# Four node-graph pairs beside the last sort and four in two alternating series after it

## The chip, the cores and the metric

The kernel runs on one core of a Trainium2 chip. The metric is the device time of one execution in microseconds (us); lower is better. The engines named here are PE (TensorE: matmuls, and PEld for the loads of their weights), DVE (VectorE), ACT (ScalarE), POOL (GpSimd, which also issues indirect DMAs) and SP (SyncE, which issues most plain DMAs).

## What is computed

There are 16 graphs of 1024 nodes with 64 channels, an adjacency matrix for each, and a node mask. Two layers follow each other, each with a residual. Cut to what matters:

```python
# layer 0
h = relu(layernorm(x))
# drop some neighbours of nodes with many, then for every node and channel
# sort the values of its neighbours and take three quantiles:
agg = sum(w * quantile(sorted_neighbours(h), tau) for tau, w in ((.25,.25), (.5,.5), (.75,.25)))
x = x + (relu((h + agg) @ W1 + b1) @ W2 + b2) * nodemask
# layer 1
h0 = relu(layernorm(x))
for i in (1, 2, 3):                      # three graph convolutions
    h_i = bn_i(relu(adj @ (h_{i-1} @ W_i) + b_i))
x = x + relu(concat(h_1, h_2, h_3) @ Wl + bl)
```

The expensive part is the sort of the neighbours' values. Layer 1 multiplies by the whole adjacency matrix of a graph three times.

## The kernel before

**Pairs and stages.** Two graphs of 64 channels fill the 128 partitions, so the 16 graphs are eight pairs, 0 to 7. For every pair, `prepare` turns the adjacency into lists of live neighbours, and puts the nodes in an order of their number of neighbours (`place` is that order). Nodes of similar number make a block; there are seven blocks (0 to 6) and the last 16 nodes, the tails, which are sorted for several pairs at once (`sort_tails`: here for pairs 4 to 7 together). `gather_block` brings a block's neighbour values with one-hot matmuls on PE (pg, L1018) whose right-hand sides s are compared on DVE (L987); ACT copies the result (g, L1023). `sort_block` sorts with minima and maxima on DVE (L935 to L950) and sums the quantiles into agg. `store` transposes the sums on PE (pt_agg, L1043), copies them on ACT (o, L1051) and writes them to the DRAM tensor agg_d (L1053).

**The later layers.** The rest of layer 0 and the whole of layer 1 are `later`, which is a generator: it yields between pieces, and whoever steps it decides where in the program's order its next piece lies. For a pair p it consists of two parts.

- `first(p)`, five steps. It loads xt (L1240) and h (L1241) with DMAs of SP, brings agg back in the nodes' own order with 16 indirect gathers of POOL, 128 rows each (L1243), and loads the mask bytes mk (L1249). Then `first_layer` adds agg and h on DVE (L1142), transposes on PE (pt, L1131), multiplies by W1 and W2 (pm L1151, py L1155), adds bias, mask and residual (h L1156, L1158, L1159), runs layer 1's layernorm on DVE and ACT (L560 to L568), and transposes again.
- `second(p)`, eleven steps. It loads the pair's two adjacency matrices (adjT, L1259, from SP), and `next_layer` does the three convolutions. For each it multiplies by W_i (pw, L1184) and splits the result into three bf16 parts (xw, L1185 to L1190). Two halves of 48 matmuls by the adjacency follow (pg, L1200), each with its relu on ACT (xT, L1204) and scaling on DVE (xT, L1205). The last linear layer is pf (L1216), then bias (L1220), relu and residual (res, L1223), and the store to out (L1225).

Within `later`, the steps of second(p) and first(p+1) alternate. All its tiles come from a pool "late" with one buffer each (only xt has two), and a PSUM pool with two buffers of each of its two tags.

**The order of the work.** Each engine works in program order. `weave` walks the sort's steps and, by the share of the sort that is done, steps other generators between them. While the sorts of pairs 0 to 6 run, these others are the preparation of the next pair and the gathers of the next block. The sort of pair 7, the last, has nothing left to prepare, so `later` runs there: in each of the seven blocks and the final one, `weave` spends STEPS = 7 steps of `later`, 56 in all. That is 5 for first(0), 3×16 for second(0) to second(2) with the first parts of pairs 1 to 3, and three steps of second(3). Between block 0 and block 1 the tails of pairs 4 to 7 are sorted, with block 1's gathers beside them. After the last sort `send` stores the last sums, and `ahead.rest()` does what remains of `later`, in the same order and the same pools. A check on inputs out of the usual (a flag, from L1504) ends the program.

Of the kernel before, what the change touches and what calls it, by code (L numbers as in the profile page):

```python
# [19 lines left out]
PSUM = bass.MemoryType.PSUM  # L20
# [8 lines left out]
TAUS = ((0.25, 0.25), (0.5, 0.5), (0.75, 0.25))  # L29

SHARES = (10, 9, 17, 24, 20, 13, 0)
STEPS = 7

MAGIC = 8388608.0

# [366 lines left out]
def graph_layers_kernel(ctx: ExitStack, tc: tile.TileContext, ins, out: bass.AP):  # L402
# [6 lines left out]
    NP = NB // 2  # L409
# [144 lines left out]
    def rows_of(ap):  # L554
        return ap.rearrange("(t p) c -> p t c", p=P)
# [550 lines left out]
    def weave(sort, *others):  # L1106


        share, taken = 0.0, [0] * len(others)

        def due(share):
            for i, (steps, count, first, end) in enumerate(others):
                while taken[i] < count and first + (end - first) * taken[i] / count <= share:
                    steps.step()
                    taken[i] += 1

        due(0.0)
        for part in sort:
            share += part
            due(share)  # L1120
        due(1.0)
# [15 lines left out]
    def first_layer(pools, xt, h, agg, mask):  # L1137


        one, ps = pools  # L1140
        X = xt.shape[2]
        nc.vector.tensor_tensor(agg, agg, h, ALU.add)  # L1142
        oT = channels_first(pools, agg, "chan")
        yield
        for x in range(X):
            rows = slice(x * C, (x + 1) * C)
            hT = one.tile([HID, N], F32, tag="hT", name="hT")
            for hf in range(NH):
                sl = slice(hf * HALF, (hf + 1) * HALF)
                pm = ps.tile([HID, HALF], F32, tag="mm", name="pm1")  # L1150
                nc.tensor.matmul(out=pm, lhsT=w1[rows, :], rhs=oT[rows, sl], start=True, stop=True)  # L1151
                nc.scalar.activation(hT[:, sl], pm, AF.Relu, bias=b1)
            py = ps.tile([P, NT, C], F32, tag="mm", name="py")
            for t in range(NT):
                nc.tensor.matmul(out=py[:, t, :], lhsT=hT[:, t * P : (t + 1) * P], rhs=w2, start=True, stop=True)  # L1155
            nc.vector.tensor_tensor(h[:, :, x, :], py, b2[:, None, :].to_broadcast([P, NT, C]), ALU.add)  # L1156
            yield
        nc.vector.tensor_tensor(h, h, mask[:, :, :, None].to_broadcast([P, NT, X, C]), ALU.mult)  # L1158
        nc.vector.tensor_tensor(xt, xt, h, ALU.add)  # L1159
        flat = "p t x c -> p (t x) c"  # L1160
        layernorm_relu(one, agg.rearrange(flat), xt.rearrange(flat), h.rearrange(flat), NT * X)
        yield
        return channels_first(pools, agg, "chan")
# [61 lines left out]
            nc.sync.dma_start(out=rows_of(graphs[x]), in_=res[:, :, x, :])  # L1225
        yield

    def later(pools, done):

        one, ps = pools  # L1230

        def first(p):
            assert p < done.sent
            xt = one.tile([P, NT, 2, C], F32, tag="xt", bufs=2, name="xt")
            h, agg = (one.tile([P, NT, 2, C], F32, tag=k, name=k) for k in ("h", "agg"))
            mk = one.tile([P, NT, 2], U8, tag="mk", name="mk")
            mask = one.tile([P, NT, 2], F32, tag="mask", name="mask")
            for x in range(2):
                b = 2 * p + x
                nc.sync.dma_start(out=xt[:, :, x, :], in_=rows_of(x_d[b]))  # L1240
                nc.sync.dma_start(out=h[:, :, x, :], in_=rows_of(h_d[b][:, :]))  # L1241
                for t in range(NT):
                    nc.gpsimd.indirect_dma_start(  # L1243
                        out=agg[:, t, x, :],
                        out_offset=None,
                        in_=agg_d[b][:, :],
                        in_offset=bass.IndirectOffsetOnAxis(ap=place[:, b, t : t + 1], axis=0),
                    )
                nc.sync.dma_start(out=mk[:, :, x], in_=mask_d[b])  # L1249
            yield  # L1250
            nc.vector.tensor_copy(mask, mk)
            cur = yield from first_layer(pools, xt, h, agg, mask)
            return xt, cur

        def second(p, x2, cur):
            adjT = []
            for x in range(2):
                adjT.append(one.tile([P, NT, N], F8, tag=f"adjT{x}", name=f"adjT{x}"))
                nc.sync.dma_start(out=adjT[x], in_=adjT_d[2 * p + x][:, :, :])  # L1259
            yield  # L1260
            yield from next_layer(pools, [out[2 * p], out[2 * p + 1]], adjT, x2, cur)

        given = yield from first(0)
        for p in range(NP):
            now = Steps(second(p, *given))
            ahead = Steps(first(p + 1)) if p + 1 < NP else None
            while now.step():
                yield
                if ahead is not None and ahead.step():
                    yield  # L1270
            if ahead is not None:
                ahead.rest()
                given = ahead.result
# [146 lines left out]
    with ExitStack() as stack:  # L1420
        keep = stack.enter_context(tc.tile_pool(name="keep", bufs=1))
        pools = (
            stack.enter_context(tc.tile_pool(name="work", bufs=1)),
            stack.enter_context(tc.tile_pool(name="ps", bufs=1, space=PSUM)),
            stack.enter_context(tc.tile_pool(name="rows", bufs=1)),
        )
        last = len(BLOCKS)
        with ExitStack() as inner:
            early = (
                inner.enter_context(tc.tile_pool(name="early", bufs=1)), keep,  # L1430
                inner.enter_context(tc.tile_pool(name="ps_early", bufs=1, space=PSUM)),
            )
            ahead = Steps(prepare(0, early))
            ahead.rest()
            st = ahead.result
            first, *_ = gather_block(st, 0, pools)
            first.rest()
            for p in range(NP - 1):


                def coming(st, p):
                    yield from st.number
                    return (yield from prepare(p + 1, early))

                ahead = Steps(coming(st, p))
                for n in range(last):
                    steps = (ahead, SHARES[n], 0.0, 1.0)
                    if n == 0 and p in TAILS:

                        tails = sort_tails(*TAILS[p], pools)  # L1450
                        next(tails)
                        weave(sort_block(st, n, pools), steps)
                        weave(tails, gather_block(st, n + 1, pools))
                    elif n == last - 1:
                        ahead.rest()
                        to_come = ahead.result
                        weave(sort_block(st, n, pools), gather_block(to_come, 0, pools))
                    elif n == last - 2:
                        weave(
                            sort_block(st, n, pools), gather_block(st, n + 1, pools),  # L1460
                            gather_block(st, last, pools, (early[0], "a", 2)), steps,
                        )
                    else:
                        weave(sort_block(st, n, pools), gather_block(st, n + 1, pools), steps)
                st = to_come
            for _ in st.number:
                pass


        with ExitStack() as inner:  # L1470
            one = inner.enter_context(tc.tile_pool(name="late", bufs=1))
            late = (one, inner.enter_context(tc.tile_pool(name="ps_late", bufs=2, space=PSUM)))
            done = Pair()
            done.sent = TAILS[NP - 1][0]
            ahead = Steps(later(late, done))
            for n in range(last + 1):
                steps = (ahead, STEPS, 0.0, 1.0)
                if n == 0:
                    tails = sort_tails(*TAILS[NP - 1], pools)
                    next(tails)  # L1480
                    weave(sort_block(st, n, pools), steps)
                    weave(tails, gather_block(st, n + 1, pools))
                    continue
                if n < last:
                    weave(sort_block(st, n, pools), gather_block(st, n + 1, pools), steps)
                else:
                    weave(sort_block(st, n, pools), steps)
                done.sent = NP - 1
            send(pools)
            done.sent = NP  # L1490
            ahead.rest()


    with ExitStack() as stack:
# [43 lines left out]
```

## Time and profile before

| What | Value |
|---|---|
| Runs | 3160.47, 3166.65, 3176.45 us, median 3166.65 |
| The profiled execution | 3163.56 us, its span 3161.8 us |
| Mean granted clock of TensorE | 0.915 of full |
| PE busy over the span | 2599.2 us (82%) |
| DVE busy over the span | 2559.8 us (81%) |
| ACT / POOL busy | 1696.2 / 619.5 us |
| Last sort (pair 7), from its first work to its last sum | 2376.6 to 2832.1 us of the span |
| Residual stores' last operation (L1223) of pairs 0 to 7 | 2622.5, 2734.9, 2821.7, 2898.8, 2971.5, 3046.9, 3107.6, 3153.7 us |
| The convolutions' matmuls (L1200) | 2304 matmuls, 284.5 us busy |
| The gathers of agg (L1243) | 128, 171.2 us busy |

Busy shares are means over the whole span; the change touches only the last quarter of it, so the table's positions matter more than its shares. Times of single operations are their start on the span's clock. A wait in the profile is put down to the one thing that came last.

### The profile page before, as it was taken

The numbers are of one execution on the slowest core, as the hardware profiler recorded it, in microseconds if no ns is written. First come the engines' busy times: TensorE is split into PE (matmuls) and PEld (weight loads), VectorE is DVE, ScalarE is ACT, GpSimd is POOL, SyncE is SP. The second block draws the span as 40 slices with busy tenths as digits, with TensorE's granted clock in tenths as the row PEclk, the third lists the DMA queues.
The fourth block names the chain that finished last, engine by engine and source line by source line (L and its number), as shares of the span: only waits on it lengthen the run. The fifth ranks groups of instructions, "written<-read, shape, count | busy, mean of one in ns | idle before, by whom it ended". The sixth has DMA issues, their size and how long they took to land.

```text
span 3161.8 us, 67201 instructions
## 1 busy us (share of the span) xinstructions
PE 2599.2 (82%) x27849; PEld 1697.4 (54%) x27849; DVE 2559.8 (81%) x5895; ACT 1696.2 (54%) x3292; POOL 619.5 (20%) x545
## 2 busy tenths in 40 slices
PE   2678978898888889885798889888986688977778
PEld 1445655565556556653565566456643456644445
DVE  4149889998999799989998999899976979963332
ACT  4764666567557755774367557745853223332221
POOL 5110161022102200330022103300422530311110
PEclk9779999999899999997899999999987799988989
DMA  4131022111211212122111211211113011122211
GB/s 138 46 104 60 3 67 70 56 55 52 66 57 54 64 56 68 46 72 47 42 64 51 66 56 57 67 56 63 48 36 75 9 41 26 49 55 54 54 54 42
DMA packets 221082, 177.45 MB, mean 56 GB/s; under 512 B 189024, under 2 KB 189152, under 8 KB 216672
## 3 DMA queue, kind: packets, MB, share of 16 engines
q1 hardware_dynamic: 141824, 125.88, 13.1%
q0 software_dynamic: 17408, 37.81, 3.9%
q10 hardware_dynamic: 61536, 9.39, 1.7%
q8 instruction: 219, 3.59, 0.5%
q14 instruction: 95, 0.78, 0.1%
HBM read 124.44 MB, written 48.55 MB: 55 GB/s over the span
## 4 chain that ended last, share of the span: by engine, by line
DVE 40%; PE 29%; ACT 12%; DMA 8%; issue 6%; another core or an unknown queue 2%; POOL 2%; ACTq 1%; DVEq 0%; POOLq 0%; SPq 0%
PE pg L1018 11%; DVE t L935 10%; DVE s L987 9%; DVE g L935 8%; PE pg L1200 5%; ACT junk L770 3%; DMA a<-in_adj 3%; DMA lp<-live_d 3%; DVE junk_v L673 2%; PE pr L845 2%; DVE g_tails L935 1%; DVE t_tails L935 1%; PE keys L763 1%; PE pf L1216 1%
## 5 line engine op out<-in xcount | busy, mean ns | idle before, releaser
L1018 PE MATMUL pg<-s,hp 128*64 128x400 bf16 (+11 forms) x16848 | 1366.5, 313 | 172.3 <-DVE s L987 138.1
L1018 PEld LDWEIGHTS <-hp 128*64 128x64 bf16 x16848 | 894.5, 112 | 553.9 <-issue 109.6
L987 DVE TENSOR_SCALAR s<-r 128x3200 bf16<-128x3200 bf16 (+25 forms) x1312 | 623.6, 521 | 103.6 <-PE pg L1018 74.9
L778 POOL DMA_INDIRECT live_d<-edge,place x128 | 261.1, 2040 | 1354.3 <-DVE place L773 1149.9
L1023 ACT COPY g<-pg 128x400 f32<-128x400 f32 (+10 forms) x384 | 169.0, 443 | 399.4 <-PE pg L1018 363.1
L935 DVE TENSOR_TENSOR t<-g 128x600 f32<-128x600 f32 (+9 forms) x524 | 315.5, 626 | 34.0 <-ACT g L1023 33.2
L1200 PE MATMUL pg<-adjT,xw 128*64 128x512 fp8e4 x2304 | 284.5, 398 | 52.8 <-ACT xw L1185 25.7
L935 DVE TENSOR_TENSOR g<-t 128x96 f32<-128x96 f32 (+16 forms) x555 | 283.2, 537 | 1.2
L1243 POOL DMA_INDIRECT agg<-agg_d,place x128 | 171.2, 1338 | 495.2 <-PE pt L1131 258.2
L671 ACT ACTIVATE edge<-a 128x1024 fp8e4<-128x1024 f32 x128 | 135.1, 1058 | 214.4 <-DMA a<-in_adj 213.9
L1200 PEld LDWEIGHTS <-xw 128*64 128x64 bf16 x2304 | 140.1, 114 | 182.4 <-issue 42.0
L868 ACT ACTIVATE coef<-z,bias 128x200 f32<-128x200 bf16 (+6 forms) x480 | 173.9, 405 | 102.3 <-DVE agg L950 66.0
L935 DVE TENSOR_TENSOR t<-t 128x192 f32<-128x192 f32 (+20 forms) x447 | 207.8, 475 | 0.2
L871 ACT ACTIVATE coef<-coef,wcol 128x200 f32<-128x200 f32 (+7 forms) x512 | 189.6, 403 | 9.3 <-issue 7.1
L673 DVE SCALAR_TENSOR_TENSOR junk_v<-a 128x1024 fp8e4<-128x1024 f32 x128 | 155.4, 1214 | 24.4 <-DMA a<-in_adj 24.4
L845 PE MATMUL pr<-liveT,upto 128*128 128x512 fp8e4 (+2 forms) x384 | 127.4, 350 | 53.1 <-ACT r L851 46.9
L770 ACT ACTIVATE junk<-keys,minus 128x1024 fp8e4<-128x1024 f32 x128 | 144.3, 1128 | 38.1 <-PE keys L763 34.3
L851 ACT CAST r<-pr 128x592 bf16<-128x592 f32 (+1 forms) x256 | 142.5, 585 | 41.1 <-PE pr L847 32.1
L794 POOL DMA_DIRECT2D lp<-live_d x128 | 89.4, 699 | 376.9 <-PE pt L809 319.3
L812 ACT ACTIVATE liveT<-pt 128x1024 fp8e4<-128x1024 f32 x128 | 130.3, 1034 | 50.5 <-PE pt L809 47.1
L752 ACT ACTIVATE edge<-q,bias 128x1024 fp8e4<-128x1024 f32 x128 | 141.8, 1108 | 22.6 <-PE q L747 22.6
L725 ACT ACTIVATE stays<-cs,back 128x1024 f16<-128x1024 f32 x128 | 136.7, 1111 | 31.1 <-PE cs L721 15.9
(182 smaller groups left out, 3879.4 us busy)
## 6 DMA issues: line engine op xcount, KB each, us to landing
a<-in_adj SPq DMA_DIRECT2D x128, 512.0 KB
adjT_d<-edgeT SPq DMA_DIRECT2D x16, 1024.0 KB
lp<-live_d POOLq DMA_DIRECT2D x128, 128.0 KB
adjT<-adjT_d SPq DMA_DIRECT2D x16, 1024.0 KB
room<-in_x SPq DMA_DIRECT2D x16, 256.0 KB
h_d<-room SPq DMA_DIRECT2D x16, 256.0 KB
h_again<-h_d SPq DMA_DIRECT2D x16, 256.0 KB
xt<-in_x SPq DMA_DIRECT2D x16, 256.0 KB
```

Of the source, the lines that this page charges most:

```text
L673: nc.vector.scalar_tensor_tensor(junk, a, 1.0, a, ALU.is_equal, ALU.not_equal, accum_out=odd[:, b, t : t + 1], saturate=False)
L770: nc.scalar.activation(junk, keys, AF.Sign, bias=minus[:, t : t + 1], accum_out=above[:, t : t + 1], saturate=False)
L778: sent = nc.gpsimd.indirect_dma_start(out=live_d[b][:, :], out_offset=bass.IndirectOffsetOnAxis(ap=place[:, b, t : t + 1], axis=0), in_=ed ...
L845: nc.tensor.matmul(out=pr[:, o], lhsT=upto, rhs=liveT[:, u, sl], start=True, stop=(u == 0))
L868: nc.scalar.activation(coef[:, i, :], z[:, at], AF.Abs, bias=bias(rank - (slots + 1) // 2 + tau), scale=sign)
L871: nc.scalar.activation(coef[:, i, :], coef[:, i, :], AF.Relu, bias=wcol[:, q : q + 1], scale=-w)
L935: nc.vector.tensor_tensor(view(bufs, o, n1, n2), view(bufs, a, n1, n2), view(bufs, b, n1, n2), ALU.max if op else ALU.min)
L987: nc.vector.tensor_scalar(s[:, k, :, us, w0:], r[:, :, us, at + w0 : at + W], float(LIVE + 1 + k0 + k), None, ALU.is_equal)
L1018: summed = nc.tensor.matmul(out=pg[x * C : (x + 1) * C, ks, w0:], lhsT=st.hp[:, part, x, u, :], rhs=s[:, ks, x, u, w0:], start=(whole and ...
L1023: nc.scalar.copy(g[:, k0 : k0 + n, :], pg)
L1200: nc.tensor.matmul(out=pg[cs, :], lhsT=part[:, u, cs], rhs=adjT[x][:, u, sl], start=(u == 0 and k == 0), stop=(u == NT - 1 and k == len(xw ...
L1243: nc.gpsimd.indirect_dma_start(out=agg[:, t, x, :], out_offset=None, in_=agg_d[b][:, :], in_offset=bass.IndirectOffsetOnAxis(ap=place[:, b ...
```

## The change

Two constants, `later`'s arguments and the end of the program change:

- `later` gets a list of pairs. Beside the last sort it runs pairs 0 to 3 (BESIDE = 4), in the order that it had.
- STEPS is 9, but block 0 gets one step only. That is 1 + 7×9 = 64 steps, which are the 5 + 3×16 + 11 of four whole pairs.
- After the last sort's stores, all pools of the sort and of these pairs are closed. New pools are opened, "last" with two buffers of each tile and "ps_last" with four buffers of each of its two tags, and `later` runs there with `apart` on.
- With `apart` two generators are made, one for pairs 4 and 6 and one for pairs 5 and 7. Each does first(p) and second(p) of its pairs one after the other, and they are stepped in turn, one step each.

```diff
-STEPS = 7
+STEPS = 9
+
+BESIDE = 4
...
-    def later(pools, done):
+    def later(pools, done, pairs, apart=False):
...
-        given = yield from first(0)
-        for p in range(NP):
+        def in_turn(pairs):
+            for p in pairs:
+                yield from second(p, *(yield from first(p)))
+
+        if apart:
+            both = [Steps(in_turn(pairs[k::2])) for k in range(2)]
+            while any([one.step() for one in both]):
+                yield
+            return
+        given = yield from first(pairs[0])
+        for p in pairs:
             now = Steps(second(p, *given))
-            ahead = Steps(first(p + 1)) if p + 1 < NP else None
+            ahead = Steps(first(p + 1)) if p + 1 in pairs else None
...
-            ahead = Steps(later(late, done))
+            ahead = Steps(later(late, done, range(BESIDE)))
             for n in range(last + 1):
-                steps = (ahead, STEPS, 0.0, 1.0)
+
+                steps = (ahead, STEPS if n else 1, 0.0, 1.0)
...
             send(pools)
-            done.sent = NP
             ahead.rest()
+
+
+    with ExitStack() as stack:
+        done.sent = NP
+        late = (
+            stack.enter_context(tc.tile_pool(name="last", bufs=2)),
+            stack.enter_context(tc.tile_pool(name="ps_last", bufs=4, space=PSUM)),
+        )
+        Steps(later(late, done, range(BESIDE, NP), True)).rest()
```

## The prediction

> **What bounds the kernel now.** I first read busy times by stage (columns: stretch, its length, busy time and count of PE, PEld, DVE, ACT, POOL, then granted PE clock, DMA share, GB/s). The last sort runs from 2376.6 to 2832.1, its last store's transpose pt_agg starts at 2832.4, and the span ends at 3161.8. That split carries the sum below.
>
> ```profile
> 2376.60:2440.60 64.00, 41.50 (x271) 24.16 (x267) 37.92 (x50) 17.08 (x42) 18.36 (x16) 0.65 0.45 84
> 2440.60:2491.00 50.40, 18.27 (x179) 13.76 (x177) 50.40 (x207) 12.60 (x44) 37.04 (x15) 0.68 0.10 22
> 2491.00:2527.80 36.80, 36.30 (x369) 23.05 (x367) 36.52 (x53) 12.29 (x28) 3.59 (x2) 0.97 0.04 3
> 2527.80:2606.00 78.20, 69.66 (x772) 47.25 (x767) 56.90 (x80) 21.63 (x47) 26.66 (x16) 0.98 0.12 28
> ...
> 2863.00:2885.00 22.00, 9.69 (x47) 4.63 (x49) 4.38 (x6) 3.10 (x5) 10.34 (x11) 0.63 0.08 18
> 2885.00:3155.00 270.00, 230.40 (x1817) 145.96 (x1813) 87.71 (x123) 64.51 (x104) 30.21 (x32) 0.93 0.19 54
> ```
>
> Rows 1 and 2 are block 0 and the tails of the sort, rows 3 and 4 blocks 1 and 2; in rows 1 and 2 PE is much idle, in row 3 PE and DVE are both full. After the sort (last two rows) PE is busy 85% and DVE 32%: PE is the bound there, except in row 5, the gather of one pair. In steps of 5 us:
>
> ```profile
> 2865.00:2870.00 5.00, 1.42 (x8) 1.12 (x8) 0.57 (x1) 0.69 (x1) 3.78 (x5) 0.87 0.12 26
> 2870.00:2875.00 5.00, 2.34 (x9) 0.72 (x9) 1.38 (x2) 1.20 (x2) 3.78 (x5) 0.50 0.12 26
> 2875.00:2880.00 5.00, 0.09 (x2) 0.09 (x4) 0.11 (x1) 0.59 (x1) 1.08 (x2) 0.50 0.06 13
> 2880.00:2885.00 5.00, 5.00 (x24) 2.04 (x26) 2.31 (x3) 0.62 (x1) 0.00 (x0) 0.50 0.00 0
> ```
>
> Here PE starves (about 11 us lost) and its clock halves. Why the gather is late stands in the waits of 2832 to 3156, and what it does beside the sort in those of 2376 to 2832 (engine, line and what it waited for: us, times, longest):
>
> ```profile
> POOL agg L1243 <- PE pt L1131: 167.9, 3, 57.9
> ```
> ```profile
> DVE agg L1142 <- DMA agg<-agg_d,place: 22.6, 2, 12.6
> ```
>
> POOL waits until a pair's transposes pt free the only agg tile; then its 16 gathers start, too late for the next pair's first layer. The tail thus costs 77.1, 72.7, 75.4, 60.7 and 46.1 us from one res (L1223) to the next (2821.7, 2898.8, 2971.5, 3046.9, 3107.6, 3153.7): 46.1 is a pair alone, 60.7 adds a first layer (14.6), 75 adds a late gather (about 15).
>
> **What the skill says.** (1) "TensorE: Matmul & The Clock Gate", Part 1: an array idle for a window of about 3.4 us drops to half clock and needs as much busy time to return. The trace agrees: 0.50 after 2870. (2) "DMA: Bandwidth & Descriptors", SWDGE vs HWDGE vs iDMA: software on GpSimd writes the descriptors of GpSimd's DMAs, in SBUF, where DVE can lock it out. In the trace one gather is 0.94 us busy with 0.30 us between (16 take 20 us) in the tail, but a group beside the sort takes 29 to 45 us, single ones up to 10.3. (3) "Trainium Architecture — The Big Picture", Inside one NeuronCore: each engine has its own stream, meeting others at semaphores. A wait thus holds everything behind it; L1142 waiting 12.6 us for a gather is that. (4) "Trainium Kernel Development and Optimization", Best Practices: double-buffer to overlap DMA with compute. The single agg agrees with the need; whether it helps depends on what runs meanwhile.
>
> **The change, part by part.** The instruction order of the changed program shows that it does what it says: pairs 0 to 3 end with the sort (64 steps = 5 + 3×16 + 11; before 56, which stopped inside pair 3), then two series alternate on PE in groups of 48 matmuls. Five places move time.
>
> A. *Block 0 gets one step.* The one step issues pair 0's loads and gathers; mask and L1142 still stand in block 0 on DVE, but pair 0's first-layer PE work and layernorm leave it. Before, L1142 ran at 2415.1 (gathers 2390.5 to 2413.4), and the block ended at 2440.3. Behind L1142, the sort needs only 5.4 us of coefficient work: end about 2421.7, **−18.6**.
>
> B. *Tails.* Three layernorm operations (1.22 each) go: 3.65 of an all-DVE stage (50.40 of 50.40): **−4.0** with their waits.
>
> C. *Block 1.* Pair 0's layernorm (six operations of about 1.2, 7.1 us) comes here, and pair 1's gathers, which wait for pair 0's transposes, can start only near 2500 where before they ran under the tails. With the 27.5 us of a disturbed group they land near 2530, while DVE reaches L1142 of pair 1 near 2513; behind it stand the s operations (L987) that PE needs, so both stop: 17 us. Two further steps bring PE about 9 us. 17+7+9 = **+33**. Bounds: 16 if the gathers take 20 us and half the PE work fits; 50 for a 45 us group.
>
> D. *Blocks 2 to 7*, 304.4 us before. Half a pair more: 195 pg matmuls at 10.6 us per 96 are 21.6, pw 4: 25.6 us of PE work at 85% (PE was 87% busy here): +22. Pair 2's late gather (12.6) goes, pair 3's now meets DVE: about +16, by the nearest waits (12.6, and C). Sum **+25**; bounds +4 (work fits in the 40 us of idle PE, gathers cancel) and +42. So pt_agg comes at 2832.4−18.6−4+33+25 ≈ **2868**.
>
> E. *After the sort.* 329.4 us before. The new pools take the room of all older ones, so the first loads and the 32 gathers of pairs 4 and 5 wait for the last stores (o, agg_d): about 3.5 us after pt_agg. Call this G.
> - 32 gathers × 1.25 = 40, landing 46. Only pair 3's last work covers (pg 10.6, pf 5.6). PE's order puts pair 5's transposes among pair 4's first layer, so both wait for both gathers. Then two first layers with nothing beside: pair 0's took 37 us from L1142 to first xw at a low clock; two overlap in about 37. pg of pair 4 starts at G+**83**.
> - Seconds of 4 and 5: two of 3×10.6 + 2×2.0 + 5.6 = 41.4 are 83, the waits at layer ends hidden by the other series. But L1142 of pair 7 stands on DVE ahead of pair 4's second half of a layer (L1205); 32 gathers again take 40, DVE is released about 17 after PE wants it. 83+17+3 = **103**.
> - First layers of 6 and 7: both series are in the same phase, nothing lies beside: **38**.
> - Seconds of 6 and 7: 83+3 = **86**; res 2; out DMA to the end 7 (3154.9 to 3161.8 before), flag chain L1504 about 1: **10**.
> 3.5+83+103+38+86+10 = 323.5: **−6**. Bounds: −55 (second item's 17 and third item's 38 hidden) and +30 (groups of 32 at beside-the-sort pace).
>
> DMA queues: SP issues the same xt, h, mk, adjT and out transfers; adjT L1259 has a second buffer and comes earlier, priced nothing because pg never shows it as a releaser. Sizes don't change. PSUM gets four buffers for two: nothing, since both series use two each. ACT goes from 24% busy in the tail and is no bound.
>
> Sum: −18.6−4+33+25−6 = **+29** on the span of 3161.8, so 3191. The profiled execution took 3163.6, and its like after the change 3193; the median of the three shown, 3166.65, lies 3 higher (3160 to 3176), so I predict **3195**. About 0.5%, 16 us, is what a measurement of this kernel can tell from no change.
>
> **Rivals.**
> *1. No difference.* D fits into PE's idle time (+4 for +25) and C's gathers take 20 (−7): 3195−28 = **3167**. For it: PE is idle 42 us in blocks 1 to 7. Against it: DVE is full in several of those blocks (45.50 of 45.50 in 2659.8 to 2705.3), so idle PE time is largely waiting that added DVE work lengthens.
>
> *2. Faster: the second series really covers the first.* Place: the end of the seconds of 4 and 5. If the transposes of 6 and 7 run under those seconds, as "ahead" did before, and DVE isn't held by L1142, 17+38 = 55 go: **3140**. It decides when more than 45 of those 55 are hidden. For it: before, next pairs' first layers cost 14.6 each in place of 37. Against it: the two series are at the same step always, so both are in first layers together.
>
> *3. Much slower: gathers.* 32 in a row at the pace of pair 1's group beside the sort (45 us for 16) would cost some 40 more in the tail or in C and D: **3230**. For: single gathers of up to 10.3 us. Against: the tail's DVE is mostly idle, and there 16 took 20 us three times.
>
> *4. It does not do what it says.* One series is held by the other's tiles, as with one buffer; about 3195 + 2×15 = 3225, folded into 3.
>
> **How the numbers follow.** Main case 0.46 (3180 to 3212), rivals 3 and 4 0.23, rival 1 0.18, rival 2 0.13. The range 3156 to 3234 takes in the bounds of C and D, all of rival 1 and most of rival 3, leaving out rival 2 and a little. Same sign: slower by over 0.5% is main and rival 3, 0.69; same 0.18; faster 0.13.
>
> **What would show it.** Pair 0's L1142 near 2415 and block 0's end near 2422 (A); L1142 of pair 1 waiting about 17 on its gather (C); pt_agg at 2855 to 2885 (D); the first gather of the last pools 3 to 5 after it, then a stretch of 60 to 80 us with PE under 40% busy at half clock, and a second one of some 40 us (E). It is wrong if pt_agg stays near 2835, or if gathers of 6 and 7 are never a releaser of DVE, or if PE is over 85% busy from pt_agg+90 to the end.

## The result, and the profile after

The changed kernel took 3177.38 us (median of 12 runs, 3164.47 to 3190.50) against 3166.95 for the kernel before (12 runs, 3149.85 to 3180.10). The ratio is 1.0028, 95% interval 1.0004 to 1.0051: some 9 us slower, where 29 were forecast, and 3195. The direction was right, but barely: the interval begins at 1.0004, and a later group of runs gave 1.0013 (0.9993 to 1.0032). The size forecast was three times too large. Some 9 us is less than the 16 that the prediction held for the least that can be told from no change.

The profiled execution took 3174.97 us, its span is 3173.2. First its busy times by stage (stretch, length, busy time and count of PE, PEld, DVE, ACT, POOL, granted PE clock, DMA share, GB/s), from the last sum ahead of block 0 on: block 0, the tails, blocks 1 and 2.

```profile
2371.00:2416.50 45.50, 24.34 (x187) 13.33 (x189) 31.63 (x42) 14.36 (x37) 19.20 (x16) 0.66 0.59 115
2416.50:2461.30 44.80, 26.62 (x217) 17.22 (x215) 44.80 (x199) 11.41 (x41) 0.00 (x0) 0.72 0.01 2
2461.30:2523.40 62.10, 40.45 (x422) 26.42 (x420) 45.42 (x64) 16.24 (x38) 19.12 (x16) 0.79 0.10 19
2523.40:2575.50 52.10, 51.70 (x549) 37.79 (x546) 51.15 (x69) 16.72 (x35) 0.55 (x1) 1.00 0.07 12
```

Block 0 is short and block 1 long, as steps A and C said: PE is idle 21.65 of block 1's 62.10 us, 16.3 of them behind DVE, which waits for pair 1's gathers. Then the same view after the sort:

```profile
2855.00:2880.00 25.00, 5.78 (x15) 4.11 (x15) 1.23 (x1) 0.00 (x0) 19.21 (x20) 0.50 0.26 68
...
2942.00:2964.00 22.00, 6.12 (x12) 1.27 (x10) 1.23 (x1) 0.00 (x0) 16.09 (x17) 0.50 0.12 26
2964.00:3033.00 69.00, 67.17 (x578) 37.28 (x578) 17.66 (x28) 16.66 (x28) 0.00 (x0) 0.94 0.07 25
...
3062.00:3073.00 11.00, 0.59 (x3) 0.59 (x4) 10.93 (x13) 2.42 (x3) 0.00 (x0) 0.59 0.00 0
```

Rows 1 and 2 lie beside 32 gathers each; a stretch in which PE gets little done is called a bubble here. Row 4 is the layernorm of pairs 6 and 7 with nothing beside it: DVE full, PE empty. Row 3 shows what two series do when nothing disturbs them: PE is 97% busy. The surprise is in row 2. PE is not stopped there: it starts 12 matmuls in 22 us, none of which needs a gather. The waits after the sort (engine, line and what it waited for: us, times, longest) say the same:

```profile
ACT xT L1206 <- remote: 77.5, 2, 40.2
PEld L1202 <- issue: 38.9, 35, 2.7
PEld pf L1218 <- issue: 29.1, 23, 2.5
DVE agg L1144 <- DMA agg<-agg_d,place: 27.0, 2, 14.0
```

"issue" is time in which PE waited for nothing that the profile shows, and "remote" a signal whose sender it does not show. Beside the gathers PE's instructions, matmuls and weight loads, start in multiples of 0.70 us after one another (2950.91, 2952.31, 2953.01, 2954.41, ...), and the half layers' completions reach ACT late (first line). I call this the **crawl**.

Both kernels had a second profile taken in a later group of runs (before_again, after_again). With all four, the prediction's steps measure as follows. Block ends are starts of the last sum (L950, after the change L952); "last store" is pt_agg.

| Step | Forecast | First pair of profiles | Second pair |
|---|---|---|---|
| A, block 0 | -18.6 | 60.3 to 45.5: -14.8 | 60.2 to 44.8: -15.4 |
| B, tails | -4 | 50.6 to 44.8: -5.8 | 50.5 to 44.9: -5.6 |
| C, block 1 | +33 | 36.6 to 62.1: +25.5 | 43.2 to 62.5: +19.3 |
| D, blocks 2 to 7, to the last store | +25 | 305.0 to 311.7: +6.7 | 304.2 to 298.2: -6.0 |
| E, from there to the end | -6 | 329.3 to 338.1: +8.8 | 323.3 to 325.8: +2.5 |
| Sum | +29 | +20.4 | -5.2 |

The sums of single profiles scatter (before_again was a long execution of its group, 3157.4 against a median of 3135.8), so the ratios above stand for the whole. Even the stretch ahead of block 0, where all the kernels of this document do the same work, took 2347.6 to 2389.6 us in the twenty profiles; in the two pairs it was 9.0 and 12.4 us shorter in the changed kernel. The steps repeat better, and D was missed in both pairs. Its rows, before and after, first pair and then second:

```profile
2527.50:2832.50 305.00, 263.07 (x2570) 177.90 (x2567) 252.59 (x727) 98.57 (x250) 66.96 (x48) 0.93 0.17 44
2523.40:2835.10 311.70, 274.38 (x2689) 186.89 (x2685) 255.84 (x732) 99.71 (x249) 36.44 (x32) 0.94 0.14 38
```
```profile
2528.10:2832.30 304.20, 256.94 (x2584) 177.57 (x2580) 252.27 (x728) 98.52 (x250) 75.81 (x48) 0.93 0.17 44
2514.00:2812.20 298.20, 270.09 (x2690) 184.64 (x2687) 256.07 (x732) 99.67 (x249) 39.74 (x32) 0.97 0.15 40
```

The crawl lies in D too. Block 3, with pair 2's gathers at its start, took 68.5 us in the first profile of the changed kernel and 54.5 in the second:

```profile
2575.50:2644.00 68.50, 53.84 (x554) 39.41 (x553) 48.70 (x82) 17.21 (x40) 15.20 (x16) 0.88 0.20 57
2566.30:2620.80 54.50, 50.55 (x554) 37.17 (x553) 48.91 (x82) 17.16 (x40) 18.54 (x16) 1.00 0.26 71
```

### The profile page after: what moved, and what is told of

The parts are those of the page before. It is cut to its first block, busy times and chain, and to the rows that moved or that the text cites. A ratio compares the mean times of both kernels' runs of the same rounds, so it can differ in the third digit from the quotient of the medians.

```text
span 3173.2 us, 67188 instructions
## 1 busy us (share of the span) xinstructions
PE 2586.3 (82%) x27826; PEld 1694.7 (53%) x27849; DVE 2559.2 (81%) x5895; ACT 1693.6 (53%) x3292; POOL 588.9 (19%) x545
## 4 chain that ended last, share of the span: by engine, by line
DVE 43%; PE 29%; ACT 11%; issue 7%; DMA 7%; POOL 2%; ACTq 1%; another core or an unknown queue 1%; DVEq 0%; POOLq 0%; SPq 0%
DVE t L937 11%; PE pg L1020 10%; DVE s L989 10%; DVE g L937 9%; PE pg L1202 6%; ACT junk L772 3%; DVE junk_v L675 3%; DMA a<-in_adj 3%; DMA lp<-live_d 2%; PE pr L847 2%; DVE g_tails L937 1%; DVE t_tails L937 1%; ACT r L853 1%; DVE coef L943 1%; PE keys L765 1%
## 5 line engine op out<-in xcount | busy, mean ns | idle before, releaser
L1202 PE MATMUL pg<-adjT,xw 128*64 128x512 fp8e4 x2304 | 277.3, 388 | 44.5 <-issue 28.5
L1246 POOL DMA_INDIRECT agg<-agg_d,place x128 | 137.0, 1070 | 475.9 <-DVE xw L1192 131.7
L1206 ACT ACTIVATE xT<-pg,c_L_gnn_b 128x512 f32<-128x512 f32 x48 | 32.9, 686 | 253.0 <-PE pg L1202 170.9
L1207 DVE TENSOR_SCALAR xT<-xT,bn_s,c_L_gnn_be 128x512 f32<-128x512 f32 x48 | 26.2, 545 | 163.3 <-ACT xT L1206 159.6
```

What stands on the lines that cost most here:

```text
L1202: nc.tensor.matmul(out=pg[cs, :], lhsT=part[:, u, cs], rhs=adjT[x][:, u, sl], start=(u == 0 and k == 0), stop=(u == NT - 1 and k == len(xw ...
```

## The experiments

They ran in groups; the kernels of a group shared a chip and the runs of the kernel before. Its median was 3163.06, 3161.44, 3135.78, 3140.09 and 3125.08 in the five groups, which ran on chips 12, 5, 6, 6 and 1. Theory W is the prediction's: PE loses time where an instruction waits for a late gather. Theory C: a gather also slows PE's other work.

**Group 1: does a gather cost PE time when nobody waits for it?** spare_gathers adds to the changed kernel, in second(p) after the adjT loads:

```diff
+            if p >= NP - 2:
+                spare = one.tile([P, NT, 2, C], F32, tag="agg", name="agg")
+                for x in range(2):
+                    for t in range(NT):
+                        nc.gpsimd.indirect_dma_start(
+                            out=spare[:, t, x, :],
+                            out_offset=None,
+                            in_=agg_d[2 * p + x][:, :],
+                            in_offset=bass.IndirectOffsetOnAxis(ap=place[:, 2 * p + x, t : t + 1], axis=0),
+                        )
```

> The changed kernel with 32 more indirect gathers, issued at the start of the last two convolution parts (pairs 6 and 7) into agg tiles that are free by then; nothing reads them, so no wait for them stands before any work. Theory C (crawl): while POOL issues gathers, PE is fed only about one instruction per 0.70 us, whoever waits for whom, from about 8 us after the first gather to the last; PE should then crawl for about 30 of the 40 us that the gathers take, inside the stretch where PE was 80.65 of 81 us busy, and the kernel should take 20 to 33 us longer than the changed one (3197 to 3210). Theory W (waits, as the prediction had it): PE loses only what stands behind the addition of agg on DVE; then nothing changes (3174 to 3181) and PE stays near 80 of 81 busy there.

Measured: 3217.88, ratio to before 1.0159 (1.0129 to 1.0190). From pair 5's res to pair 7's it took 147.5 us, against 118.0 in the changed kernel: 29.5 for 32 gathers. (The rest of the difference lies in the first bubble, which was 12 longer here.) Busy times beside the spare gathers:

```profile
3100.00:3110.00 10.00, 10.00 (x76) 7.97 (x76) 6.21 (x9) 6.34 (x12) 7.66 (x7) 0.83 0.10 21
3110.00:3120.00 10.00, 6.46 (x48) 2.59 (x45) 0.84 (x2) 0.69 (x1) 7.56 (x9) 1.00 0.13 26
3120.00:3130.00 10.00, 5.08 (x12) 0.85 (x11) 0.00 (x0) 0.00 (x0) 7.56 (x9) 0.52 0.13 28
3130.00:3140.00 10.00, 2.45 (x5) 0.77 (x6) 0.00 (x0) 0.00 (x0) 7.56 (x9) 0.50 0.12 26
```

The gathers start at 3100.5. PE keeps its rate for some 10 us, then falls from 76 matmuls in 10 us to 5. Nothing waits for these gathers, so theory W can't explain the loss; theory C can.

plain_loads puts SP loads in the place of the last four pairs' gathers:

```diff
+                    if p >= BESIDE:
+                        nc.sync.dma_start(out=agg[:, t, x, :], in_=agg_d[b][t * P : (t + 1) * P, :])
+                        continue
```

> The changed kernel with the 64 gathers of pairs 4 to 7 replaced by 64 plain loads of SP of the same size; it leaves out the putting back of the sums in the nodes' own order for these pairs. It gives the whole price of the gathers after the sort. Theory C: both crawls (2848 to 2884 and 2942 to 2964 in the changed kernel) vanish, and the stretch from the last pt_agg to the end falls from 338 to about 280 (33 of the first bubble, 21 to 30 in the first pair of convolutions): 3115 to 3125. Theory W: the first bubble shrinks by about 30, the second stall by the 17 predicted: 3128 to 3135.

Measured: 3134.08, ratio 0.9891 (0.9858 to 0.9924). From the last store to the end 292.8 instead of 338.1. Gathers cost 45 us there. The total is what W expected, but its parts fit neither theory: the first bubble gained only 8 us, where both had some 30 (the loads of xt and h and the first layers remain there), and the seconds of pairs 4 and 5 fell by 34.7, from 115.7 to 81.0, where W had 17 and C 21 to 30.

old_tail keeps the changed steps beside the sort, and takes the old order and pools after it:

```diff
-            ahead = Steps(later(late, done, range(BESIDE)))
+            ahead = Steps(later(late, done, range(NP)))
...
+            done.sent = NP
             ahead.rest()
...
-        Steps(later(late, done, range(BESIDE, NP), True)).rest()
```

> The changed steps beside the sort (one step in block 0, then nine) with the old order after it: one series through all eight pairs in the old single-buffer pools. If the extra half pair beside the sort is nearly free (sort stretch from block 0's store to pt_agg +12 in the changed kernel's profile) and the loss lies after the sort, this is 329 less 36 for half a pair after the sort, so about 25 us faster than before: 3138 to 3150. If the sort stretch pays for the half pair in full when pair 4's first part also runs beside it, it comes out level: 3160 to 3172.

Measured: 3169.26, ratio 1.0016 (0.9999 to 1.0034); of the two outcomes expected, the level one came, and not a gain of 25 us. The sort's stretch grew by 14.6 (452.5 to 467.1) and the rest shrank by 11.1 (329.3 to 318.2). Busy times of the two stretches, first of the kernel before, then of old_tail:

```profile
2380.00:2832.50 452.50, 357.62 (x3353) 238.05 (x3354) 373.77 (x1026) 140.05 (x362) 125.95 (x80) 0.86 0.19 44
2832.50:3161.80 329.30, 266.35 (x2065) 166.21 (x2064) 105.51 (x150) 75.55 (x123) 45.30 (x48) 0.90 0.18 49
```
```profile
2371.60:2838.70 467.10, 372.06 (x3423) 245.30 (x3424) 376.46 (x1029) 141.61 (x365) 91.56 (x80) 0.86 0.19 43
2838.70:3156.90 318.20, 259.10 (x1996) 163.04 (x1995) 103.49 (x147) 73.34 (x119) 45.74 (x48) 0.89 0.19 51
```

PE is busy 14.4 us more beside the sort, and the stretch is 14.6 longer. In this pair of profiles the 95 us in which PE was idle there before took up none of it in sum. The second pair shows the opposite, though: from before_again to after_again PE's work in this stretch grew by 11.3 us (351.01 to 362.30), and the stretch shrank by 7.7 (458.1 to 450.4). And old_tail's block 3 holds the crawl (68.1 us). So what PE work beside the sort costs is not shown.

one_series runs pairs 4 to 7 in the new pools, but in the old alternation (`apart` off).

> The changed kernel, but pairs 4 to 7 after the sort in one series as before (the convolutions of a pair in turn with the next pair's first layer), in the new two-buffer pools. Theory C: the first bubble is 20 us shorter (one pair's gathers), then periods of about 75, 75, 61 and 46 us: 325 to 332 from pt_agg to the end instead of 338, so 3165 to 3173. Theory W: with two buffers the gathers are early enough to hide, periods of 61, 61, 61, 46: about 300, so 3137 to 3145.

Measured: 3190.75, ratio 1.0080 (1.0052 to 1.0107), slower than two series and than both theories said. With two buffers, pair 5's gathers follow pair 4's at once, so the first bubble (2850 to 2890) has 32 gathers here too; in it PE was busy 14.19 of 40.00. In the stretches with the gathers of pairs 6 and 7 PE was then busy 10.62 of 23.00 and 53.52 of 67.00 us. The expectation had taken one pair's gathers for the first bubble.

**Group 2: which transfers do it, and is an earlier gather worth it?** spare_pool_plain has `nc.gpsimd.dma_start` from rows as they lie for the spare gathers.

> As spare_gathers, but the 32 spare transfers are plain DMAs of POOL (128 rows of 256 bytes, rows as they lie) instead of indirect ones. If it is the indirect gather that slows PE, the time stays at the changed kernel's 3174 to 3181. If any unbroken run of DMAs that POOL issues does it, PE crawls here too, and it is 20 to 38 us over the changed kernel (3197 to 3216).

Measured: 3186.16, ratio 1.0079 (1.0053 to 1.0104), over the time expected for no effect; its first bubble was 12 us longer (100 from the last store to pair 6's first gather, against 88). From pair 5's res to pair 7's it took 117.9. Rows beside the kernel's own gathers of pairs 6 and 7 (first two), and beside the spare plain transfers (last two):

```profile
2955.00:2960.00 5.00, 3.11 (x12) 0.76 (x10) 0.00 (x0) 0.00 (x0) 3.78 (x5) 0.50 0.13 26
2960.00:2965.00 5.00, 2.21 (x6) 0.39 (x4) 1.22 (x1) 0.00 (x0) 3.78 (x5) 0.50 0.14 26
...
3098.00:3103.00 5.00, 5.00 (x50) 2.61 (x48) 2.76 (x5) 1.97 (x4) 5.00 (x11) 1.00 0.21 60
3103.00:3108.00 5.00, 5.00 (x50) 2.61 (x46) 0.55 (x1) 0.51 (x2) 4.38 (x9) 1.00 0.24 67
```

In one execution PE crawls beside indirect gathers and not beside plain DMAs of POOL of the same 128 rows of 256 bytes, though POOL is as busy. The plain ones were over in 17 us, so this shows 7 us past the time at which the crawl sets in.

spare_paced issued the spare gathers three at a time behind small POOL copies.

> As spare_gathers, with the same 32 indirect gathers, but issued three at a time, each three after a POOL copy of 16 numbers of the half layer (xT) that has just been finished, so about 3.75 us of gathers in every 5 to 7 us. Theory C1: only an unbroken run over about 8 us slows PE; then the spare gathers are nearly free: 0 to 8 us over the changed kernel (3177 to 3186). Theory C2: each gather costs PE its 1.2 us wherever it lies: 3210 to 3220 as in spare_gathers.

Measured: 3203.68, ratio 1.0116 (1.0082 to 1.0151), and 142.4 between the two res. It tells nothing on pacing: the gathers did not wait for the copies on POOL, and ran 25 and 7 in a row.

sums_early changes the kernel before: `fetch(p)` holds the 16 gathers, agg has two buffers, and fetch(p+2) is issued at the start of second(p).

```diff
-        res = one.tile([P, NT, X, C], F32, tag="res", name="res")
+        res = one.tile([P, NT, X, C], F32, tag="hT", name="res")
...
+        def fetch(p):
+            assert p < done.sent
+            agg = one.tile([P, NT, 2, C], F32, tag="agg", bufs=2, name="agg")
+            for i in range(2 * NT):
+                x, t = divmod(i, NT)
+                nc.gpsimd.indirect_dma_start(
+                    out=agg[:, t, x, :],
+                    out_offset=None,
+                    in_=agg_d[2 * p + x][:, :],
+                    in_offset=bass.IndirectOffsetOnAxis(ap=place[:, 2 * p + x, t : t + 1], axis=0),
+                )
+            yield
+            return agg
...
+        sums = [Steps(fetch(p)) for p in range(NP)]
+        sums[0].rest()
+        sums[1].rest()
+        given = yield from first(0, sums[0].result)
...
             while now.step():
+                if p + 2 < NP:
+                    sums[p + 2].step()
```

> The kernel before, with two agg buffers in the old pool (res takes hT's place in SBUF), and pair p+2's 16 gathers issued in one run at the start of pair p's convolutions, a whole pair ahead of their use; nothing else moved. Theory W (a late gather is waited for, as the prediction read the kernel before): periods after the sort of 75 become 61, and the two waits of DVE beside the sort (10.0 and 12.6) go: 3163 - 42 - 20, so 3095 to 3115. Theory C (a run of gathers takes PE's time wherever it lies beside PE work): the crawl only moves, so 3150 to 3170.

Measured: 3141.27, ratio 0.9913 (0.9879 to 0.9948): between the two theories. sums_paced, whose copies again did not hold the gathers apart (16 ran in a row), was its twin: 3132.03, 0.9887 (0.9853 to 0.9922).

> As sums_early, but three gathers at a time, each three after POOL has read the last finished half layer. Theory C1: the crawls go (three of about 12 us after the sort, some of the stalls beside it): 3105 to 3130. Theory C2: as sums_early.

**Group 3: pacing held by data, and second profiles.** In spare_paced2 and sums_paced2 POOL first copies 16 numbers of the half layer just finished into the slice that the gather then fills, so the order is kept:

```diff
+                        nc.gpsimd.tensor_copy(spare[:1, t, x, :16], seen)
```

> As spare_paced, but the pacing is now held by data: POOL copies 16 numbers of the half layer just finished into each of the three slices of the spare tile, and only then gathers into them (in spare_paced the copies had been put behind the gathers, which ran in a row). From the second pair's res before (L1225 of pair 5) to that of pair 7 the changed kernel took 118.0 us, spare_gathers 147.5, spare_paced 142.4. Theory C1 (only an unbroken run over about 8 us slows PE): 118 to 124. Theory C2 (each gather costs PE its time wherever it lies): 140 to 150.

> sums_early with the pacing held by data in the same way, at most six gathers in a row. sums_early took 3141 and its unpaced twin sums_paced 3132. Theory C1: the two crawls left after the sort (about 9 to 16 us each) and most of those beside it go: 3100 to 3120. Theory C2: 3130 to 3145.

> The changed kernel once more, for a second profile. The stretch from block 0's store to the last pt_agg was 464.1 in its first profile and 461 to 464.2 in three variants that share it; the one from pt_agg to pair 6's first gather was 87.8 in its first profile and 88 to 100 in variants that share it. If that is its spread, the whole from block 0's start to the end is 795 to 815, and the ratio to before stays within 1.000 to 1.007.

> The kernel before once more, for a second profile. Its stretch from block 0's first sum to the last pt_agg was 452.5 and from there to the end 329.3. If both repeat within 3 us, the difference of 20 us between the first two profiles is the change's, and what is left to the ratio of 1.003 lies in the spread of the runs ahead of it; if the sum comes out 10 us longer, the first profile of before was a short one.

Measured: spare_paced2 3137.35, ratio 1.0007 (0.9988 to 1.0026), 117.0 between the two res; sums_paced2 3071.43, ratio 0.9805 (0.9778 to 0.9832); after_again 3140.92, ratio 1.0013 (0.9993 to 1.0032); before_again 3157.4 once. Two expectations of repeats failed: after_again took 776.2 us from block 0 to the end, not 795 to 815, and before_again's two stretches moved by 5.6 and 6.0 us, not by under 3. The paced runs looked like the proof of pacing. But after_again, which paces nothing, did not crawl either. Rows beside the gathers of pairs 6 and 7 (2903.6 to 2944.1), where the first profile fell from 16 to 2 matmuls in 5 us:

```profile
2913.00:2918.00 5.00, 5.00 (x50) 2.62 (x48) 0.00 (x0) 0.69 (x1) 3.77 (x4) 1.00 0.15 30
2918.00:2923.00 5.00, 5.00 (x50) 2.64 (x48) 0.00 (x0) 0.69 (x1) 3.78 (x4) 1.00 0.15 26
2923.00:2928.00 5.00, 5.00 (x50) 2.64 (x48) 2.24 (x3) 0.69 (x1) 3.88 (x4) 1.00 0.13 26
2928.00:2933.00 5.00, 2.68 (x24) 1.56 (x20) 0.05 (x1) 1.27 (x2) 3.78 (x4) 1.00 0.12 26
2933.00:2938.00 5.00, 0.00 (x0) 0.00 (x0) 0.00 (x0) 0.00 (x0) 3.78 (x4) 0.76 0.14 26
```

PE runs at full rate beside the gathers, until it truly waits (last row): that is the standstill behind L1144 of pair 7 that step E of the prediction forecast.

**Group 4: the crawl itself.** Four of these kernels once more, on one chip.

> spare_gathers once more, on the same chip as the next three. In the last runs (after_again, spare_paced2, sums_paced2) PE kept its full rate of about 56 instructions in 3 us beside gathers, and the kernel before took 3136 instead of 3163, so the crawl may belong to some executions or chips, not to every one. From pair 5's res to pair 7's (118.0 in the changed kernel): about 147 if this one crawls, 117 to 119 if it doesn't.

> spare_paced2 once more. Where spare_gathers2 crawls, it tells the theories apart: 117 to 124 from pair 5's res to pair 7's if pacing prevents the crawl (C1), 140 to 150 if each gather costs its time (C2). Where spare_gathers2 doesn't crawl, both take 117 to 119, and the crawl is a matter of the execution.

> sums_early once more, beside sums_paced3. Where nothing crawls, theory W has its full value: the gathers are a pair ahead, so periods after the sort of 61 and a ratio to before of about 0.980, as sums_paced2 had. Where gathers in a row crawl, about 0.990 as in its first run.

> sums_paced2 once more. C1: 0.978 to 0.983 whether the others crawl or not. If its 0.9805 came from a chip without the crawl alone: 0.985 to 0.992 where the others crawl, and equal to sums_early2 where they don't.

Measured: spare_gathers2 3139.65, ratio 0.9998 (0.9973 to 1.0023), 117.0 between the two res: the spare gathers, not paced, cost nothing. A row beside them:

```profile
3060.00:3070.00 10.00, 10.00 (x98) 5.22 (x94) 1.09 (x2) 1.37 (x2) 7.56 (x9) 1.00 0.15 28
```

spare_paced3 0.9989 (0.9973 to 1.0004), 117.1. sums_early2 3061.61, ratio **0.9746** (0.9713 to 0.9779); sums_paced3 3071.94, ratio 0.9785 (0.9753 to 0.9817). So the crawl belongs to some executions or some chips, pacing is worth nothing without it, and without it an early gather has theory W's full value and more (0.980 was expected). In sums_early2's waits after the sort, addition L1142 waits for h, not for a gather:

```profile
DVE agg L1142 <- DMA h<-h_d: 4.9, 3, 1.7
```

From res to res it takes 60.7, 61.2, 59.2 and 46.1 (pairs 4 to 7).

**Group 5** repeats the paced kernels on another chip, and they did not crawl there: PE started 50 matmuls in 5 us beside the unpaced gathers of spare_paced4, which took 3123.43 once and 117.1 between the two res. sums_paced4 took 3067.85, ratio 0.9782 (0.9732 to 0.9833).

> spare_paced2 once more. Its own gathers of pairs 6 and 7 lie beside PE work in a row, so its trace shows by itself whether this execution crawls there. If it crawls: 117 to 124 us from pair 5's res to pair 7's if pacing prevents the crawl (C1), 140 to 150 if each gather costs its time (C2). If it doesn't crawl: 117, and this stays open.

> sums_paced2 once more. If spare_paced4 crawls: a ratio of 0.978 to 0.983 by C1, about 0.990 (as sums_early had where it crawled) by C2. If not: 0.978 to 0.983 by both.

Nine of the ten profiles of the first result and of groups 1 and 2 show PE slowed beside gathers after the sort (the tenth, plain_loads, has none there). In the old order that shows less in spaced instructions than in finished work of PE that ACT takes up late, as in the kernel before:

```profile
ACT xT L1204 <- remote: 29.3, 3, 11.7
```

None of the ten profiles of groups 3 to 5 is slowed so. Waits put down to "remote" part the two kinds throughout: they stand beside the sort, and already ahead of it, in all ten of the first kind, plain_loads too, and nowhere in the ten others. Block 3 of the changed order took 67.4 to 68.5 us in the seven profiles of the first kind that have it, and 54.4 to 55.7 in the five of the second. What differs between the executions is not shown. Groups 1 and 2 ran on chips 12 and 5, groups 3 to 5 on 6 and 1 (that of the first result is not on record). No chip is known to have shown both kinds, so it may be the chip. Whether pacing prevents the crawl stays open.

## Why the prediction was wrong in size

**A and B held** within 4 us. L1142 of pair 0 came 1.7 us later than forecast, seen from the first gather on (26.3 after it, 24.6 before); the rest of A's miss is the sort's own work behind it.

**C was too high**: 33, and 19 to 25 came. The wait of DVE for pair 1's gathers, priced at 17, measured 16.3. The rest is DVE's own: it was full in block 1 before (36.32 of 36.60 us), and after the change it is busy 45.42, which with the wait are 61.7 of the block's 62.10. Its added work, the layernorm above all, was thus 9.1 us, where 7 were priced. The two extra steps of PE, priced at another 9, added nothing of their own beside a DVE that was full. (In the second pair C is smaller because in before_again DVE was idle 6.8 us of block 1 already.) The prediction's "29 to 45 us" for a group of gathers beside the sort also left out two of the five groups before, of 23 and 20 us; pair 1's took 24 here, where 27.5 were assumed.

**D is the step that failed**: 25, and 7 or -6 came, although the 7 hold some 14 us of crawl in block 3 that no term had. It was a sum of two terms, both mis-sized.
- PE work. Priced at 25.6 us, of which 22 were to show. The convolutions in blocks 2 to 7 did grow, by 186 matmuls pg (846 to 1032) against the 195 forecast. But the stage also lost work that I had not counted: 93 of the sort's own matmuls (1274 to 1181). 87 of them are block 2's gathers pg L1018, 6.8 us of PE's busy time, which now ran in block 1, nearly all of them before DVE's wait there. PE's busy time from block 1's end to the last store rose only from 263.07 to 274.38, by 11.3 (13.2 in the second pair). Nor did that work show in the length: in the second pair PE's idle time in the stage fell from 47.3 to 28.1.
- Waits for gathers. Priced at +16 for pair 3 and -12.6 for pair 2. In the first pair of profiles 12.6 went and 12.0 came; in the second the kernel before waited three times, 33.3 in all, and the changed one once, 12.0. The 21 us that went outweigh the 13.2 of added PE work there, which is how D can be negative.

The prediction had named a sign against itself, a last store that stays near 2835. It came at 2835.1, or 2844.1 with the 9.0 us by which this execution was shorter ahead of block 0, and not at 2855 to 2885. Rival 1 (3167, no difference) came nearer than the main case. Its reason was that idle PE time takes up D's work; the second pair fits that and old_tail's profile doesn't, so it stays open. The changed kernel gains 21 in block 0 and the tails and pays 19 to 25 for it in block 1.

**E came out right in its sum where PE does not crawl, and not where it does.** Its items, forecast, first profile, second profile:

| Item | Forecast | First (crawl) | Second (none) |
|---|---|---|---|
| last store to pg of pair 4 | 86.5 | 92.8 | 96.5 |
| convolutions and pf of pairs 4 and 5 | 103 | 115.7 | 100.7 |
| first layers of 6 and 7 | 38 | 37.0 | 36.0 |
| convolutions and pf of 6 and 7 | 86 | 81.0 | 81.0 |
| to the end | 10 | 11.6 | 11.6 |
| Sum | 323.5 | 338.1 | 325.8 |

Even the second sum owes something to luck: its first item was forecast 10 us too small, and the others together 8 too large. The last pools' first gather started 4.8 and 5.2 us after the last store, where 3.5 were forecast. In the first profile the first and third items, 93 and 37 us, leave PE idle for 40 and 11 us. That E's miss in the first profile, +14.8, makes up for most of D's, -18.3, is luck too. Of the second item's 103, 20 us were forecast as a standstill of PE behind L1142 of pair 7. That is 18 us in the second profile and 33 us, a crawl, in the first. The clue stood in the profile of the kernel before: among the waits after its sort, L1142 never waits for a gather, though PE stands still beside each of them. I quoted the 22.6 us of such waits from beside the sort and took the standstill after it for the same thing. In before_again, which does not crawl, L1142 does wait there, 33.0 us in three times, and that stretch was only 6 us shorter (323.3 for 329.3). That fits a crawl that in the old order fell mostly where PE would have waited anyway. In the new order PE has work beside the gathers of pairs 6 and 7, and the crawl costs more.

On the Trainium skill's "TensorE: Matmul & The Clock Gate", Part 1: the half clock is in both bubbles here too (0.50 in 2855 to 2880 and 2942 to 2964), but it explains a factor of two, not 5 matmuls in 10 us. "Trainium Kernel Development and Optimization", Best Practices, tells to double-buffer: sums_early does that for the one tile that made gathers late and gains 0.9 to 2.5%; the changed kernel doubled every tile after the sort and gained nothing. That its order puts little beside the gathers of pairs 4 and 5 is a likely reason, not one that a run here separates.

## What to carry to other kernels

Before moving work under another stage, count what that stage already does in each of its blocks, which engine is full there, and what leaves them: the moved work's length mattered less here than which waits came and went, and PE's added steps beside a full DVE cost nothing of their own. Look for the one tile whose single buffer makes a transfer late, and give that one a second buffer and an earlier issue: sums_early, a local change to the kernel before, is 0.9% to 2.5% faster than it, where the larger reordering of the same work came out even. Before reading a difference of 10 us between two profiles, take both again, on another chip too: block 1 of the kernel before took 36.6 and 43.2 us in two profiles. And two series that are always in the same phase hide waits inside a phase, but not the phase itself.

## What the hardware showed that I had not expected

In some executions a run of 16 to 32 indirect gathers on POOL slowed PE, from about 10 us after its start, to one instruction in multiples of 0.70 us, with the reason "issue": 29.5 us for 32 gathers that nobody waited for. In others (on chips 6 and 1, not 12 and 5) the same gathers, in the same program, cost it nothing (117.0 and 117.1 us for the stretch with and without them). Plain DMAs from POOL, 32 in 17 us, did not slow it in an execution in which indirect ones did. The trace's packets of kind "instruction" took 1.0 and 1.3 us beside the spare gathers of spare_gathers, where PE crawled, and 1.0 to 1.3 in spare_gathers2, where it did not. A slower transfer of instructions is thus not seen, and the cause is open. The kernel before took 3161 to 3167 in the groups with the crawl and 3125 to 3140 in those without.
